# A quarter of the B products of one batch moved from GpSimd to ScalarE and TensorE

## The chip, the cores and the metric

The kernel runs on one core of one Trainium2 chip. The metric is the device time of one execution in microseconds (us). The core has five engines that run side by side, each through its own instructions in a fixed order: PE (TensorE, matrix products), DVE (VectorE), ACT (ScalarE), POOL (GpSimd) and SP (SyncE, which here only issues DMAs). They meet through semaphores.

## What is computed

The input is x, 4 batches of 384 channels by 32 by 32 pixels (1024 positions). Layer 0 normalises x and runs a selective scan over it in four directions ("turns": rows, columns, and both backwards). Layer 1 is attention with a window over the 1024 tokens of a batch and a mixture of four experts, two to a token. Cut to the scan, which is where the change lies:

```python
dts, Bs, Cs = (x_dbl[:, :, :R], x_dbl[:, :, R:R + N], x_dbl[:, :, R + N:])      # R = 12, N = 16
dts = jnp.einsum('bkrl,kdr->bkdl', dts, dt_projs_weight)
A = -jnp.exp(A_logs).reshape(K, D, N)
dt = jax.nn.softplus(dts + dt_projs_bias[None, :, :, None])
def step(h, inp):                      # over the 1024 positions
    dtt, ut, bt, ct = inp
    dA = jnp.exp(dtt[..., None] * A)
    h = h * dA + (dtt * ut)[..., None] * bt[:, :, None, :]
    y = jnp.einsum('bkdn,bkn->bkd', h, ct)
    return (h, y)
```

For each batch, direction and channel there are 16 states. A state needs a decay exp(dt A), an input dt u B, the recurrence over positions, and a product of its result with C; the products of the 16 states of a channel are then added up.

## The kernel before

**Slots.** The work of the scan is cut into 768 slots. A slot is a tile of 128 partitions by 1024 positions, and its partitions hold 32 channels by 4 states (`SG = 4`). A block is 32 channels, and takes `NG = 4` slots, one for each group g of four states. Three tiles `t` of 128 channels with four blocks `j` each make a turn: 48 slots; four turns make a batch. The slots of two neighbouring blocks alternate, so eight slots (g = 0, 0, 1, 1, 2, 2, 3, 3) belong together, and the order is the same on all engines.

**What a slot costs on each engine:**

- SP loads `spreads[n, 0]` (dt, in a `dts` buffer) and `spreads[n, 1]` (dt times u, in a `dtu` buffer), each copied to the 4 states of its channel on the way, once for a block; and rows of B and C (`bcs`), broadcast, once for a turn and g.
- ACT (`decay`): `dA = exp(dt A)`, from SBUF into a PSUM tile. There are two such tiles `das_`.
- POOL (`times_b`): `z = dtu * B`, SBUF to SBUF. There are seven `z` tiles. It may be at most `AHEAD = 3` slots ahead of the scan.
- DVE (`scan`): the recurrence, with `da` from PSUM and `z` from SBUF, in one instruction.
- DVE or POOL (`times_c`): the product with C. On POOL (`on_pool`), the scan writes into `z`, and `da` comes free at once. On DVE the scan writes into `da`, which comes free after the product.
- PE (`fold_y`): for two slots at a time, four products with `fold` add up the states. After that the two `z` come free.

**dt.** `half_step` makes dt for half of the positions of one tile: a product on PE, then softplus by ACT in pieces. Its last step adds three terms: in the first batch PE does that by three products with the identity (`by_pe`), in the others DVE by two additions. Then DVE makes dt times u, and SP stores both to DRAM (`dtr`), from where `spread` loads them.

**The rest.** When a batch has been scanned, its attention runs (`tokens`), then the routing, and the experts' blocks (`hidden`, `output`; 73 blocks in all) in three packs: batch 0, batches 1 and 2, batch 3. They share the engines with the scan of the next batches. What follows the scan of batch 3 has no scan beside it. `prepare` lays weights out afresh in DRAM during the first turns; `wts` is a stock of eight buffers for weights, which is little used in the first batch.

**Order.** All this is written as Python generators. A planner (`Machine`) with estimated costs decides, while the program is built, which instruction each engine gets next; the chip then runs these fixed lists. Ties are decided by a seeded random number (`SEED`), so a change of seed, or of any step, draws the order of the whole program afresh. `EARLY` and `LATER` are handicaps in the planner's choice.

Of the kernel before, what the change touches and what calls it, by code (L numbers as in the profile page):

```python
# [11 lines left out]
F32 = mybir.dt.float32  # L12
AF = mybir.ActivationFunctionType
ALU = mybir.AluOpType
# [375 lines left out]


PATIENCE = 3.0
TIE, SEED = 0.1, 53
SOON = 0.5
WINDOW, COLD = 3.413, 1.9
MARGIN, QUEUES = 1.0, ("sp",)
# [4 lines left out]
def conv_attn_hybrid(  # L401
# [159 lines left out]
    have = set()  # L561
    count_of = dict(scan=0, times=0)
    pe, act, dve, pool, sp = m.pe, m.act, m.dve, m.pool, m.sp

    def place_of(s):

# [100 lines left out]
    def group_norm(b):  # L667
# [91 lines left out]
        def project(pair):  # L759
            if not b and pair:  # L760
                yield lambda: count_of["times"] > 0
            xos = yield from (zs_ if b else wts).take("xo", n=2)
            given = xos
            xos = [xo[:, :L] for xo in xos]
            for h in range(NH):
                if b:
                    us = yield from us_.take("ux", n=2)
                    uv = [us[t // NH][:, ts(t % NH, HB)] for t in range(T)]
                    for t in range(T):
                        yield from sp.dma_start(uv[t], udr[b][t][:, ts(h, HB)])  # L770
                else:
                    uv = [first_u[t][:, ts(h, HB)] for t in range(T)]
                ps = yield from banks.take("ps_x", 0)
                pv = ps[: 2 * XR, :]
                mm = Calls()
                for t in range(T):
                    mm.matmul(
                        pv, xw_sb[:, t, 2 * pair : 2 * pair + 2, :].rearrange("p k r -> p (k r)"),
                        uv[t], start=t == 0, stop=t == T - 1,
                    )  # L780
                yield from pe.all(mm)
                if b:
                    us_.give(*us)
                    yield from act.copy(xos[0][: 2 * XR, ts(h, HB)], pv)
                yield from (copy if b else dve.tensor_copy)(
                    xos[1][: 2 * XR, :].rearrange("r (w h) -> r h w", h=HH)[:, ts(h, HH // NH), :],
                    pv.rearrange("r (h w) -> r h w", w=WW),
                )
                if not b:
                    yield from act.copy(xos[0][: 2 * XR, ts(h, HB)], pv)  # L790
                banks.give(ps)
            if not b and pair == 0:
                xds[0] = [xos[1][:R, ts(h, HB)] for h in range(NH)]
            for n in (1, 0):
                r = slice((1 - n) * XR, (2 - n) * XR)
                yield from sp.dma_start(xdr[b][2 * pair + n], xos[n][r, :])
                have.add(("x", b, 2 * pair + n))
            if b:
                zs_.give(*given)
            elif pair:  # L800
                wts.give(*given)
            else:
                wts.give(given[0])
                first_u.append(given[1])
# [26 lines left out]
    def state_rows(c):  # L831

        for i, (b, k) in enumerate(turns):
            for g in range(NG):
                yield lambda: ("x", b, k) in have
                bc = yield from (cs_ if c else bs_).take("bc")
                r = R + c * NS + SG * g
                yield from sp.dma_start(
                    bc, xdr[b][k, r : r + SG, :].unsqueeze(0).to_broadcast([32, SG, L])
                )  # L840
                bcs[i, g, c] = bc
# [23 lines left out]
    def half_step(i, t, h, u, dtr):  # L865
        b, k = turns[i]
        bias, c = dtb_sb[:, k, t : t + 1], ts(h, HB)
        by_pe = b == 0
        e, dt, *more = yield from eds.take("ed", n=3 if by_pe else 2)
        w = yield from banks.take("ps_dt", 0)  # L870
        yield from pe.matmul(w, dtws[i][h][:, ts(t, P)], xds[i][h], start=True, stop=True)
        yield from act.activation(e, w, AF.Abs, bias=bias)
        yield from act.activation(dt, w, AF.Relu, bias=bias)
        yield from act.activation(e, e, AF.Exp, scale=-1.0)
        if by_pe:
            yield from act.activation(w, e, AF.Identity, bias=minus, scale=-1.0)
            yield from dve.scalar_tensor_tensor(e, w, 1.0, e, ALU.add, ALU.add)
            yield from act.activation(more[0], w, AF.Ln, scale=-1.0)
            mm = Calls()
            for n, part in enumerate((dt, e, more[0])):  # L880
                mm.matmul(w, ident, part, start=n == 0, stop=n == 2)
            yield from pe.all(mm)
        else:
            yield from act.activation(w, e, AF.Identity, bias=1.0)
            yield from dve.scalar_tensor_tensor(e, w, -1.0, e, ALU.add, ALU.subtract)
            yield from act.activation(w, w, AF.Ln)
            yield from dve.tensor_tensor(w, w, e, ALU.subtract)
            yield from dve.tensor_tensor(w, w, dt, ALU.add)
        if k % 2:
            v = slice(h * (WW // NH), (h + 1) * (WW // NH))  # L890
            yield from dve.tensor_tensor(
                e.rearrange("p (w h) -> p w h", h=HH),
                w.rearrange("p (w h) -> p w h", h=HH), colmajor(u)[:, v, :], ALU.mult,
            )
        else:
            yield from dve.tensor_tensor(e, w, u[:, c], ALU.mult)
        yield from act.copy(dt, w)
        banks.give(w)
        yield from sp.dma_start(dtr[1][:, c], e)
        yield from sp.dma_start(dtr[0][:, c], dt)  # L900
        eds.give(e, dt, *more)

    def spread(c):

        for n, (i, t, j) in enumerate(blocks):
# [4 lines left out]
            )  # L910
            spreads[n, c] = dst

    def times_b():
        for s in range(NSLOT):
            n, g = place_of(s)
            i = blocks[n][0]
            yield lambda: (
                (n, 1) in spreads and (i, g, 0) in bcs and s <= count_of["scan"] + AHEAD
            )
            z = yield from zs_.take("z", 0)  # L920
            yield from pool.tensor_tensor(z, spreads[n, 1], bcs[i, g, 0], ALU.mult)
            zs[s] = z
            count_of["times"] += 1
            if g == NG - 1:
                dtus.give(spreads.pop((n, 1)))
            if n % NB == NB - 1:
                bs_.give(bcs.pop((i, g, 0)))

    def decay():
        for s in range(NSLOT):  # L930
            n, g = place_of(s)
            i, t, j = blocks[n]
            yield lambda: (n, 0) in spreads and "a4" in have
            da = yield from das_.take("dA")
            yield from act.activation(
                da, spreads[n, 0], AF.Exp, scale=a4[:, turns[i][1], t, j, g : g + 1]
            )
            das[s] = da
            if g == NG - 1:
                dts.give(spreads.pop((n, 0)))  # L940
# [14 lines left out]
    def scan():  # L955

        for s in range(NSLOT):
            n, g = place_of(s)
            i = blocks[n][0]
            yield lambda: s in zs and s in das  # L960
            z, da = zs[s], das.pop(s)
            on_pool = count_of["times"] >= min(s + AHEAD, NSLOT) and m.clock["pool"] < m.clock["dve"] + LEAD
            h = z if on_pool else da
            if turns[i][1] >= 2:
                yield from dve.tensor_tensor_scan(
                    h[:, ::-1], da[:, ::-1], z[:, ::-1], 0.0, ALU.mult, ALU.add
                )
            else:
                yield from dve.tensor_tensor_scan(h, da, z, 0.0, ALU.mult, ALU.add)
            count_of["scan"] = s + 1  # L970
            if s % SP == 0:
                m.spawn(fold_y(n), EARLY)
            if on_pool:
                das_.give(da)
                m.spawn(times_c(s, h, True))
            else:
                yield from times_c(s, h, False)
# [336 lines left out]
    def route(at_part):  # L1314
# [67 lines left out]
        nb = rp.tile([P, NE], F32, tag="nb", name="nb")  # L1382
        slot = rp.tile([P, PT, NE], F32, tag="slot", name="slot", bufs=1)
        if opens:
            total = rp.tile([P, NE], F32, tag="total", name="total")
            done = rp.tile([P, NE], F32, tag="done", name="done")
            start = rp.tile([P, NE], F32, tag="start", name="start")
            counts[PACK[b]] = total, done, start
            mm.scalar_tensor_tensor(
                slot, bcast(base_e, PT), float(P), cn[:, :PT, :], ALU.mult, ALU.add  # L1390
# [254 lines left out]
    with tc.manual_schedule():  # L1645
# [3 lines left out]
            m.spawn(group_norm(b), EARLY)  # L1649
        for gen in (turn_loads(), time_steps(), state_rows(0), state_rows(1), spread(1), spread(0)):  # L1650
            m.spawn(gen, EARLY)
        for gen in (decay(), times_b(), scan()):
            m.spawn(gen)
        m.spawn(layer1(), EARLY)
# [58 lines left out]
```

## Time and profile before

| | |
|---|---|
| time, median of 3 runs | 3725.83 us (3725.29 to 3727.22) |
| the profiled execution's own time | 3715.52 us |
| its span, first to last instruction | 3713.8 us |
| busy PE / DVE / ACT / POOL | 2999.4 / 2858.1 / 2217.3 / 2802.2 us |
| first scan / last scan ends | 61.1 us / 3029.6 us |
| turns 1 to 4 (first batch) | 167.3, 161.6, 166.6, 162.4 us |
| turns 5 to 8 (second batch) | 202.6, 213.4, 182.3, 175.7 us |
| third and fourth batch | 786.9 and 749.7 us |

The turns are read from the trace: DVE's 768 scans in order of time, 48 to a turn, from the start of a turn's first scan to the start of the next turn's. In a row of the profile stand the line, engine, operation, tiles (out<-in), shapes and count; then the busy time of the group, the mean duration of one in ns, the engine's idle time just before them, and what ended it. Most steps are recorded through one helper, so lines L155 and L166 hold nearly all, and a row is told by its tiles. An engine overlaps the end of an instruction with the start of the next, so a group's busy time over its count can be less than the mean duration.

### The profile page before, as it was taken

Reading aid. Unit: us, or ns where it says so; the run is one execution under the profiler, and the core shown is the slowest. Engines: PE = TensorE matmul, PEld = TensorE weight load, DVE = VectorE, ACT = ScalarE, POOL = GpSimd, SP = SyncE. Lnnn points to the kernel's source line nnn. Section 1 sums busy time; section 2 is a strip of 40 time slices with the busy share of each in tenths; the row PEclk is TensorE's granted clock in tenths of the full one; section 3 lists DMA queues with packets and bytes.
Section 4 is the critical chain, followed back from the end, with each engine's and each line's share of the span. In section 5 each row is a group of like instructions: output and inputs, shape, how many; then the busy total and the mean of one; then the engine's idle time right before and its main releaser. Section 6 shows DMA issues by size and latency. Waiting matters only on the chain.

```text
span 3713.8 us, 49879 instructions
## 1 busy us (share of the span) xinstructions
PE 2999.4 (81%) x15793; PEld 1820.8 (49%) x15793; DVE 2858.1 (77%) x3282; ACT 2217.3 (60%) x3984; POOL 2802.2 (75%) x1466
## 2 busy tenths in 40 slices
PE   5566565578788888896778898988888889999997
PEld 2111110045455545463445555655555558877886
DVE  4999999989888999999888999898898963331001
ACT  4454455477676777775667577876667644542221
POOL 3999988989899988999888799998899950112001
PEclk8766776688799989896778899987999999999997
DMA  5876887635489988864369999553899874469995
GB/s 201 288 279 238 276 301 251 207 124 165 150 298 347 368 323 329 304 211 151 124 218 311 328 338 347 194 178 133 291 320 328 321 262 156 153 222 321 321 322 174
DMA packets 396472, 944.51 MB, mean 254 GB/s; under 512 B 50064, under 2 KB 181256, under 8 KB 396208
## 3 DMA queue, kind: packets, MB, share of 16 engines
q1 hardware_dynamic: 384600, 915.73, 70.7%
q0 software_dynamic: 8192, 25.17, 2.0%
q8 instruction: 126, 2.06, 0.2%
q14 instruction: 138, 1.13, 0.1%
q10 hardware_dynamic: 3416, 0.41, 0.1%
HBM read 765.26 MB, written 194.77 MB: 259 GB/s over the span
## 4 chain that ended last, share of the span: by engine, by line
PE 34%; DVE 14%; ACT 10%; POOL 8%; DMA 7%; issue 6%; SPq 1%; another core or an unknown queue 1%; DVEq 0%; POOLq 0%; ACTq 0%
PE y_ff L166 9%; PE ps_hid L166 9%; POOL z L155 6%; DVE dA L155 5%; DVE z L155 4%; PE ps_y L166 3%; PE ps_qk L166 3%; ACT dA L155 2%; PE ps_pr L166 2%; DMA dtr<-ed 2%; PE ps_o L166 2%; ACT ed L155 1%; DVE ps_r L166 1%; PE ps_c L166 1%; ACT L166 1%
## 5 line engine op out<-in xcount | busy, mean ns | idle before, releaser
L155 POOL TENSOR_TENSOR z<-dts,bc 128x1024 f32<-128x1024 f32 x768 | 1792.9, 2363 | 112.5 <-PE ps_y L166 55.7
L155 ACT ACTIVATE dA<-dts,a 128x1024 f32<-128x1024 f32 x768 | 855.3, 1118 | 500.5 <-DVE z L155 486.0
L155 DVE TENSOR_TENSOR_SCAN dA<-dA,z 128x1024 f32<-128x1024 f32 x418 | 955.9, 2287 | 88.9 <-ACT dA L155 75.1
L166 PE MATMUL ps_y<-z,fold 128*32 128x512 f32 x3072 | 665.9, 732 | 321.4 <-POOL z L155 177.1
L155 POOL TENSOR_TENSOR z<-z,bc 128x1024 f32<-128x1024 f32 x350 | 821.3, 2360 | 106.7 <-DVE z L155 105.3
L155 DVE TENSOR_TENSOR_SCAN z<-dA,z 128x1024 f32<-128x1024 f32 x350 | 786.3, 2275 | 38.3 <-ACT dA L155 36.2
L166 PE MATMUL y_ff<-w_sb,hs 128*128 128x384 f32 x1752 | 671.1, 524 | 49.7 <-ACT hs L166 48.6
L166 PEld LDWEIGHTS ps_hid<-xbt,w_sb 128*128 128x128 f32 x5256 | 634.5, 196 | 131.0 <-issue 47.5
L166 PE MATMUL ps_hid<-xbt,w_sb 128*128 128x128 f32 x5256 | 658.8, 282 | 23.1 <-DMA w_sb<-wl 6.7
L155 DVE TENSOR_TENSOR z<-dA,bc 128x1024 f32<-128x1024 f32 x418 | 510.3, 1221 | 19.1
L166 PEld LDWEIGHTS y_ff<-w_sb,hs 128*128 128x128 f32 x1752 | 333.9, 204 | 297.9 <-ACT hs L166 72.9
L155 ACT ACTIVATE hs<-ps_hid,bb 128x128 f32<-128x128 f32 x876 | 262.0, 365 | 337.8 <-PE ps_hid L166 249.6
L166 PEld LDWEIGHTS ps_y<-z,fold 128*32 128x32 f32 x3072 | 91.6, 118 | 694.6 <-POOL z L155 322.9
L155 POOL DMA_INDIRECT cb<-ysdr,idx x64 | 61.9, 967 | 311.8 <-DMA ysdr<-yb 277.1
L166 POOL TENSOR_TENSOR rn<-rn,half 128x1 f32<-128x1 f32 x96 | 53.1, 553 | 229.6 <-DVE rn L166 188.3
L155 DVE COPY yb<-y_ff 128x384 f32<-128x384 f32 x23 | 12.8, 557 | 243.6 <-PE y_ff L166 242.0
L155 POOL DMA_INDIRECT xsdr<-tks,idx x64 | 65.4, 1022 | 110.0 <-DVE idx L166 48.2
L155 ACT ACTIVATE ed<-ps_dt,dtb_sb 128x512 f32<-128x512 f32 x192 | 123.5, 681 | 38.0 <-PE ps_dt L155 24.1
L155 ACT COPY ed<-ps_dt 128x512 f32<-128x512 f32 x96 | 56.2, 585 | 116.0 <-DVE ed L155 115.8
L166 PE MATMUL ps_dt<-ed,ident 128*128 128x512 f32 x144 | 82.7, 729 | 45.0 <-ACT ed L155 45.0
L155 PE MATMUL ps_dt<-xd,dtw_sb 12*128 12x512 f32 x180 | 108.7, 780 | 9.3 <-DVE gate L166 3.0
L311 ACT ACT_TABLE_LOAD x79 | 101.4, 1283 | 13.0 <-DMA gb_sb<-in_gb_dram 11.6
(220 smaller groups left out, 3509.8 us busy)
## 6 DMA issues: line engine op xcount, KB each, us to landing
w_sb<-wl SPq DMA_DIRECT2D x584, 576.0 KB
dts<-dtr SPq DMA_DIRECT2D x384, 512.0 KB
bc<-xdr SPq DMA_DIRECT2D x128, 512.0 KB
dtr<-ed SPq DMA_DIRECT2D x192, 256.0 KB
yp<-ydr SPq DMA_DIRECT2D x96, 256.0 KB
ydr<-yp SPq DMA_DIRECT2D x96, 256.0 KB
ub<-udr SPq DMA_DIRECT2D x45, 512.0 KB
xsdr<-zero SPq DMA_DIRECT2D x12, 1536.0 KB
```

The source lines that it names most:

```text
L155: return getattr(self.real, op)(*a, **k)
L166: getattr(self.real, op)(*a, **k)
L311: self.nc.scalar.add_instruction(mybir.InstLoadActFuncSet(name=self.nc.get_next_instruction_name(), act_func_set_id=EXP_LN_SET,))
```

## The change

In turns 2 to 4 of the first batch, the slots with g = 3 (36 of 768: every fourth) get their `z` in another way. `turn_inputs` loads dt times u once more as 128 channels by 1024 positions (`nat`), turns it round on PE in 128x128 pieces so that positions lie on partitions, and copies it to SBUF (`back`). There B is one number to a partition for each state, so ACT multiplies by it with its `scale` operand, 128 elements at a time, and writes the four states side by side with a step of four elements (`zt`). `decay` then has PE turn eight pieces of 128x128 back, into the PSUM tile in which the decay would have been; the decay itself is written by ACT into the SBUF tile `z`, and the scan takes its operands from the swapped places. The columns of B are made in `project`, by products with parts of the identity (`cols`). POOL's product, and the broadcast load of B for g = 3 of these turns, fall away. POOL's lead in the condition for a product with C on POOL is one slot shorter in these turns. The first tile's sums of the first turn go from PE to DVE. Three small tiles of the routing get one buffer in place of two, and the seed changes.

```diff
-TIE, SEED = 0.1, 53
+TIE, SEED = 0.1, 5
+TURNED, SOONER = 3, 24
...
+    def turned(i, g):
+
+        return 0 < i < KG and g == TURNED
...
+            if not b:
+                for n in (1, 0):
+                    k = 2 * pair + n
+                    if k == ORDER[0]:
+                        continue
...
+                    r = (1 - n) * XR + R + SG * TURNED
+                    mm = Calls()
+                    for a in range(NT):
+                        mm.matmul(
+                            ps[:, SG * a : SG * a + SG], xos[n][: 2 * XR, ts(a, P)],
+                            ident[: 2 * XR, r : r + SG], start=True, stop=True,
+                        )
+                    yield from pe.all(mm)
+                    yield from act.copy(b_cols[0][:, k * NT * SG : (k + 1) * NT * SG], ps[:, : NT * SG])
...
+                if not c and turned(i, g):
+                    continue
...
-        by_pe = b == 0
+        by_pe = b == 0 and i + t > 0
...
+    def turn_inputs():
+        for i in range(1, KG):
+            k = turns[i][1]
+            for t in range(T):
+                yield lambda: (i, t) in dtrs and ("columns", k) in have and len(dtrs) > T
+                yield lambda: count_of["scan"] >= (i * T + t) * TS - SOONER
+                nat = yield from wts.take("nat")
+                yield from sp.dma_start(nat[:, :L], dtrs[i, t][1])
+                yield m.settled(nat)
+                back = yield from wts.take("back")
+                for h in range(NH):
+                    ps = yield from banks.take("ps_tu")
+                    mm = Calls()
+                    for a in range(NT // NH):
+                        mm.transpose(ps[:, ts(a, P)], nat[:, h * HB + a * P : h * HB + a * P + P], ident)
+                    yield from pe.all(mm)
+                    yield from act.copy(back[:, ts(h, HB)], ps)
+                    banks.give(ps)
+                wts.give(nat)
+                tiles = []
+                for a in range(NT):
+                    if a % 2 == 0:
+                        z = yield from wts.take("zt")
+                        tiles.append(z)
+                    v = z[:, a % 2 * SG * P : (a % 2 + 1) * SG * P].rearrange("p (d s) -> p s d", s=SG)
+                    for n in range(SG):
+                        yield from act.activation(
+                            v[:, n, :], back[:, ts(a, P)], AF.Copy, scale=b_cols[0][:, (k * NT + a) * SG + n :][:, :1]
+                        )
+                wts.give(back)
+                across[i, t] = tiles
...
     def times_b():
...
+            if turned(i, g):
+                yield lambda: (n, 0) in spreads and (s - 2 in das or count_of["scan"] >= s - 1)
             z = yield from zs_.take("z", 0)
-            yield from pool.tensor_tensor(z, spreads[n, 1], bcs[i, g, 0], ALU.mult)
+            if turned(i, g):
+                _, t, j = blocks[n]
+                yield from act.activation(
+                    z, spreads[n, 0], AF.Exp, scale=a4[:, turns[i][1], t, j, g : g + 1]
+                )
...
     def decay():
...
+            if turned(i, g):
+                yield lambda: (i, t) in across
+                da = yield from das_.take("dA")
+                mm = Calls()
+                for a in range(NT):
+                    at = a % 2 * SG * P + j * P
+                    mm.transpose(da[:, ts(a, P)], across[i, t][a // 2][:, at : at + P], ident)
+                yield from pe.all(mm)
+                das[s] = da
...
-            on_pool = count_of["times"] >= min(s + AHEAD, NSLOT) and m.clock["pool"] < m.clock["dve"] + LEAD
+            on_pool = count_of["times"] >= min(s + AHEAD - (0 < i < KG), NSLOT) and m.clock["pool"] < m.clock["dve"] + LEAD
             h = z if on_pool else da
+            of, to = (z, da) if turned(i, g) else (da, z)
...
-            total = rp.tile([P, NE], F32, tag="total", name="total")
-            done = rp.tile([P, NE], F32, tag="done", name="done")
-            start = rp.tile([P, NE], F32, tag="start", name="start")
+            total = rp.tile([P, NE], F32, tag="total", name="total", bufs=1)
+            done = rp.tile([P, NE], F32, tag="done", name="done", bufs=1)
+            start = rp.tile([P, NE], F32, tag="start", name="start", bufs=1)
...
+        m.spawn(turn_inputs(), LATER)
```

More of the change, by code (lines that the diff above doesn't have):

```diff
@@ L791, in project @@
                 banks.give(ps)
+            if not b:
[3 more added lines that the diff above has]
+                        continue
+                    if not b_cols:
+                        b_cols.append((yield from wts.take("cols")))
+                    ps = yield from banks.take("ps_bc", 0)
+                    r = (1 - n) * XR + R + SG * TURNED
[8 more added lines that the diff above has]
+                    banks.give(ps)
+                    have.add(("columns", k))
             if not b and pair == 0:
@@ L911, in spread @@
             spreads[n, c] = dst
+    across = {}
+    b_cols = []
+    def turn_inputs():
[15 more added lines that the diff above has]
+                    yield from act.copy(back[:, ts(h, HB)], ps)
+                    banks.give(ps)
+                wts.give(nat)
[11 more added lines that the diff above has]
+                across[i, t] = tiles
+        wts.give(b_cols[0])
     def times_b():
@@ L917, in times_b @@
             yield lambda: (
-                (n, 1) in spreads and (i, g, 0) in bcs and s <= count_of["scan"] + AHEAD
+                (n, 1) in spreads and (turned(i, g) or (i, g, 0) in bcs) and s <= count_of["scan"] + AHEAD
             )
+            if turned(i, g):
+                yield lambda: (n, 0) in spreads and (s - 2 in das or count_of["scan"] >= s - 1)
             z = yield from zs_.take("z", 0)
-            yield from pool.tensor_tensor(z, spreads[n, 1], bcs[i, g, 0], ALU.mult)
+            if turned(i, g):
[3 more added lines that the diff above has]
+                )
+                if g == NG - 1:
+                    dts.give(spreads.pop((n, 0)))
+            else:
+                yield from pool.tensor_tensor(z, spreads[n, 1], bcs[i, g, 0], ALU.mult)
             zs[s] = z
@@ L925, in times_b @@
                 dtus.give(spreads.pop((n, 1)))
-            if n % NB == NB - 1:
+            if n % NB == NB - 1 and not turned(i, g):
                 bs_.give(bcs.pop((i, g, 0)))
@@ L932, in decay @@
             i, t, j = blocks[n]
+            if turned(i, g):
[7 more added lines that the diff above has]
+                das[s] = da
+                if j == JB - 1:
+                    wts.give(*across.pop((i, t)))
+                continue
             yield lambda: (n, 0) in spreads and "a4" in have
@@ L961, in scan @@
             z, da = zs[s], das.pop(s)
-            on_pool = count_of["times"] >= min(s + AHEAD, NSLOT) and m.clock["pool"] < m.clock["dve"] + LEAD
+            on_pool = count_of["times"] >= min(s + AHEAD - (0 < i < KG), NSLOT) and m.clock["pool"] < m.clock["dve"] + LEAD
             h = z if on_pool else da
+            of, to = (z, da) if turned(i, g) else (da, z)
             if turns[i][1] >= 2:
                 yield from dve.tensor_tensor_scan(
-                    h[:, ::-1], da[:, ::-1], z[:, ::-1], 0.0, ALU.mult, ALU.add
+                    h[:, ::-1], of[:, ::-1], to[:, ::-1], 0.0, ALU.mult, ALU.add
                 )
             else:
-                yield from dve.tensor_tensor_scan(h, da, z, 0.0, ALU.mult, ALU.add)
+                yield from dve.tensor_tensor_scan(h, of, to, 0.0, ALU.mult, ALU.add)
             count_of["scan"] = s + 1
```

## The prediction

> **What bounds the kernel now.** I read first the page's chain that ended last (its shares are spread over all engines: PE 34%, DVE 14%, ACT 10%, POOL 8%, so it settles nothing), then busy times by stretches, then the waits there, then the rows that price the parts.
>
> ```profile
> 228.40:390.00 161.60, 98.19 (x256) 21.15 (x252) 151.34 (x93) 78.47 (x90) 154.30 (x67) 0.67 0.74 256
> 390.00:556.60 166.60, 100.11 (x288) 23.35 (x288) 156.00 (x109) 88.61 (x100) 150.70 (x67) 0.71 0.83 284
> 556.60:719.00 162.40, 89.60 (x220) 14.31 (x220) 158.23 (x103) 79.67 (x94) 151.05 (x67) 0.65 0.67 228
> sum 490.60, PE 287.90 PEld 58.81 DVE 465.58 ACT 246.75 POOL 456.05; mean PE 95.97 PEld 19.60 DVE 155.19 ACT 82.25 POOL 152.02
> ```
> ```profile
> 1493.00:1679.30 186.30, 159.81 (x898) 98.75 (x896) 172.86 (x188) 142.29 (x262) 177.63 (x92) 0.89 0.73 253
> 2879.20:3029.60 150.40, 134.83 (x777) 82.59 (x776) 145.20 (x85) 100.26 (x162) 144.69 (x63) 0.95 0.84 298
> ```
>
> After the time, the columns are busy PE, PEld, DVE, ACT, POOL, then granted clock, DMA share, GB/s. In turns 2 to 4 (490.6 us) DVE works 94.9% and POOL 93.0% of the time, ACT only 50%. So DVE and POOL together set the pace, and the slots' C products, which either can make, level them. The last two rows are turns 9 and 16, for comparison.
>
> ```profile
> POOL z L155 <- DVE z L155: 20.5, 9, 6.5
> DVE dA L155 <- ACT dA L155: 5.2, 6, 1.7
> PE ps_y L166 <- POOL z L155: 95.5, 44, 7.1
> PE ps_dt L166 <- ACT ed L155: 14.7, 6, 4.4
> ACT dA L155 <- DVE z L155: 180.5, 102, 3.8
> ```
>
> These are waits in the same stretch (total, times, longest). POOL's waits are mostly for DVE; ACT waits 180.5 us for DVE to give a PSUM tile back. PE waits with its folds for POOL: idle time that today costs nothing.
>
> ```profile
> L155 POOL TENSOR_TENSOR z<-dts,bc 128x1024 f32<-128x1024 f32 x146 | 339.1, 2362 | 12.7 <-DMA xdr<-xo 5.9 <-PE ps_y L166 4.5 <-DMA ydr<-yd 2.3
> L155 POOL TENSOR_TENSOR z<-z,bc 128x1024 f32<-128x1024 f32 x52 | 121.5, 2355 | 21.4 <-DVE z L155 20.5 <-DVE ps_gm L166 0.9
> L155 DVE TENSOR_TENSOR_SCAN z<-dA,z 128x1024 f32<-128x1024 f32 x54 | 120.8, 2273 | 2.4 <-ACT dA L155 2.4
> L155 DVE TENSOR_TENSOR z<-dA,bc 128x1024 f32<-128x1024 f32 x92 | 112.6, 1224 | 7.7
> ```
> ```profile
> L166 PE MATMUL ps_p<-ident,s 128*128 128x128 f32 x360 | 59.4, 310 | 11.2 <-ACT pt L155 3.4 <-DVE mx L155 1.8 <-ACT yl L155 1.5
> L155 ACT ACTIVATE hs<-ps_hid,bb 128x128 f32<-128x128 f32 x876 | 262.0, 365 | 337.8 <-PE ps_hid L166 249.6 <-issue 71.0 <-remote 4.4
> L155 ACT ACTIVATE yd<-un,dsum 128x1024 f32<-128x1024 f32 x9 | 18.8, 2090 | 0.0
> L155 ACT ACTIVATE un<-un,g 128x1024 f32<-128x1024 f32 x9 | 11.2, 1239 | 10.9 <-DMA un<-in_x_dram 8.7 <-issue 2.2
> ```
>
> The first four are the prices of a B product, a C product on POOL, a scan and a C product on DVE; the last four, from the whole run, are the nearest rows for what is added.
>
> **POOL and DVE, turns 2 to 4.** POOL loses 36 B products: 36 x 2.362 = 85.0 us. The two programs' orders show what takes the place: of these turns' 144 C products DVE made 31, 31 and 29 and now makes 20, 20 and 22. So 29 go to POOL: 29 x 2.355 = 68.3 us. POOL nets 16.7 us less (439.4 busy), DVE 29 x 1.224 = 35.5 us less (430.1 busy). POOL becomes the fuller of the two. If it keeps its whole idle time (34.5 us), the stretch shrinks by 16.7; if DVE keeps its own (25.0), by 35.5. POOL's idle time is mostly waiting for DVE, which now has the room, so I let the fuller engine work the share that the fuller one works now: 439.4 / 0.949 = 463.0 us, a gain of 27.6.
>
> **ACT.** Added: 288 multiplications of 128x128. The row of hs gives 262.0 / 876 = 0.30 us each back to back and 0.365 alone; yd, which writes with a step, costs 2.090 - 1.239 = 0.851 us per 1024 elements more than un, or 0.106 per 128. So 0.30 to 0.47; I take 0.36 (the step here is four elements, yd's is 32), 104 us. With 18 copies of 128x512 at 0.585 (the row ed<-ps_dt), 10.5 us, ACT comes to 246.8 + 114 = 361 us of 463, 78% (at the bounds 74% and 85%). The 36 exponentials only change the tile that they write. In turn 9 ACT works 142.3 / 186.3 = 76%, with POOL at 95% and DVE at 93%, so this is hidden behind ACT's 180.5 us of waits for DVE; where an exponential that DVE needs comes late behind a multiplication, that costs 0.36.
>
> By the Trainium skill ("ScalarE: Activation LUTs", What ACT_TABLE_LOAD costs), an activation has a fixed price of 186 ns and 93 for a pointer operand, with 0.833 ns an element, so that cutting work into 128 elements pays mostly for the start: an estimate of 0.386 us alone, 0.29 back to back. That speaks against this form; the hs row agrees within its two readings, and 288 x 0.386 = 111 us would change the load by 7 us, still hidden.
>
> **PE.** Added: 72 + 288 transposes at 59.4 / 360 = 0.165 us, 59 us in all, 1.32 for a slot's eight. PE's 288 us leave room. What matters is the new wait: a turned slot's scan waits for its eight transposes, and these for the PSUM tile, free one scan (2.28 us) earlier, and for whatever stands before them in PE's list. In the new order a fold stands directly in front of 20 of the 36, but nearly all fold slots four or more back, or ones whose C product DVE has made. Five (three that fold a product of POOL's from three slots back, two from two back) can be late. A fold takes 1.92 us (four products at 0.48 in the timeline at 602 us), so with three hops of 0.1 between engines (as from the end of ACT's dA at 61.00 to the scan at 61.10) 1.92 + 1.32 + 0.3 - 2.28 = 1.3 us each. Behind the transposes queue the next folds, which give `z` tiles back to POOL. Three more stand behind products for dt, which wait up to 4.4 us for ACT (row ps_dt <- ACT ed). So 5 x 1.3 = 6.5, up to 6.5 + 3 x 4.4 = 20; with nothing late, 0. I take 7 us.
>
> The granted clock is 0.65 to 0.71 here. The Trainium skill ("TensorE: Matmul & The Clock Gate", Part 4: PE-mode transpose) says that transposes do not count as busy for the clock gate, so that the added work would leave the folds at 1.92 us; if it raised the clock to full, a fold would take some 0.67 x 1.92 = 1.3 us, and the 7 us would be 3.
>
> **DMA, and SP.** Nine loads of 512 KB come (nat), three of 512 KB go (B rows): 3.1 MB more, 12 us at the stretch's 256 GB/s, where DMA is busy 67 to 83%. Nine issues of 0.6 us go into SP's list ahead of some loads of dts. A slot's dtu is needed 30 slots after the load is allowed, about 96 us, so nothing: bounds 0 and 3 us. The table loads in the two orders fall from 158 to 146, 15 us of ACT over the run, hidden.
>
> **The start.** With DVE making the first sums, the wait of DVE for PE (36.11 to 40.95 us) becomes two additions of 0.69: 3.4 us earlier. But eight column products now stand on PE before the first dt product, and wait for ACT's second copy (ends 30.90, dt product now at 30.35): 16 instructions at 0.16 to 0.27 us (row ps_xt<-gw_sb) make it 3.2 to 5 us later. -0.2 to +1.6 us; I take 0.
>
> **After the first batch** everything hangs on its last fold, so the gain is carried along. The new order has 48 experts' blocks begun before the last scan, as before; so the tail, where PE is busy over 90%, has the same load. C products by DVE go from 297 to 304 there; DVE's instructions of turns 5 to 15, priced by their rows, sum to 3 us more, POOL's 7 products less. Order drawn afresh: +2, with 10 either way, for equal numbers of slots took 774, 787 and 750 us in three batches.
>
> **Sum.** -27.6 + 7 + 2 = -18.6 us. The profiled execution's 3715.5 becomes 3696.9; that execution lies 10.3 below the median of the runs, so on the median's footing 3725.8 - 18.6 = 3707. A difference under 0.2% (7.5 us) could not be told from none.
>
> **Rivals.**
>
> *Slower: PE's list holds up the scan.* If the fold in front of the transposes is late as a rule, because POOL, now the fuller engine, finishes its C products late, all 36 turned slots lose 1.3 us: 47 us; -27.6 + 47 + 2 = +21, or 3747. It decides once the mean loss passes 27.6 / 36 = 0.77 us. For it speaks PE's 95.5 us of waiting for POOL in this stretch; against it, that the folds in front are old ones. Chance 0.19.
>
> *No change: POOL keeps its idle time.* Gain 16.7 only, less 12 us of late transposes and 2 later: 3723. For it: POOL's B products still must be made ahead in slot order, and with 28 C products a turn it has no slack. Chance 0.15.
>
> *More: DVE was the pace-maker.* The stretch shrinks by DVE's 35.5, nothing is late, the new order costs nothing: 3690. For it: in turn 16 both work 96 to 97% of the time, so they can run levelled; 439.4 / 0.965 = 455 is the same gain. Chance 0.18.
>
> **How the numbers follow.** The forecast has the rest, 0.48, between about 3695 and 3716 (the two bounds of the transposes and of the redrawn order). Faster: 0.48 + 0.18 = 0.66; same 0.15; slower 0.19. The range takes in the largest gain with some of the order's 10 us, 3684, and two thirds of the way from no change to the slow rival, 3740.
>
> **What would show it.** Right: turns 2 to 4 take some 470 us; POOL 93 to 95% busy, DVE a little less, ACT near 78%; zt near 0.36 us; DVE's waits for PE at turned slots sum to under 10 us; the rest keeps its length. Wrong: a row of DVE waiting for PE's dA of tens of us; ACT's exponentials late behind zt; POOL's idle time as large as now; or later batches that differ by more than 10 us.

## The result, and the profile after

| | before | changed |
|---|---|---|
| median of 20 runs each | 3726.16 us | 3709.45 us |
| lowest to highest | 3710.31 to 3740.31 | 3697.61 to 3728.32 |
| ratio, 95% interval | | 0.9958 (0.9947 to 0.9970) |
| the profiled execution's own time | 3715.52 us | 3714.82 us |

The changed kernel is faster by 0.42%, 15.6 us; the interval spans 11 to 20 us. The forecast was 3707. The two profiled executions differ by only 0.7 us, since that of before lay 10 us under its median and that of the changed kernel 5 us over its own. So each program was profiled once more, and lengths of stretches are compared between pairs of profiles.

The changed kernel by stretches, as before: turns 2, 3 and 4 and their sum.

```profile
229.30:377.80 148.50, 95.35 (x362) 36.62 (x360) 137.59 (x82) 102.68 (x168) 146.91 (x64) 0.80 0.77 271
377.80:540.50 162.70, 111.24 (x408) 43.21 (x408) 143.61 (x99) 119.11 (x201) 145.58 (x64) 0.76 0.84 300
540.50:701.40 160.90, 98.28 (x344) 30.52 (x344) 150.07 (x95) 102.90 (x171) 152.15 (x67) 0.74 0.70 244
sum 472.10, PE 304.87 PEld 110.35 DVE 431.28 ACT 324.69 POOL 444.65; mean PE 101.62 PEld 36.78 DVE 143.76 ACT 108.23 POOL 148.22
```

Turns 2 to 4 fell from 490.6 to 472.1 us. DVE has 34.3 us less to do and POOL 11.4 us less; ACT has 78 us more. POOL is now the fuller of the two, at 94.2%. The waits in that stretch:

```profile
DVE dA L155 <- POOL z L155: 9.8, 5, 4.3
DVE ed L155 <- ACT ps_dt L155: 5.2, 4, 2.2
DVE z L155 <- PE dA L166: 5.0, 5, 1.6
DVE dA L155 <- PE dA L166: 4.9, 4, 1.5
DVE z L155 <- ACT dA L155: 4.5, 5, 1.7
```
```profile
ACT dA L155 <- DVE z L155: 61.5, 38, 7.1
PE dA L166 <- DVE z L155: 45.1, 16, 10.1
```

The new wait, DVE for the transposes (PE dA), is there twice, for scans that write `z` and scans that write `dA`: 9.9 us at 9 of the 36 turned slots. ACT's waits for DVE fell from 180.5 to 61.5 us, more than the 78 us of new work on it. The new work itself, in the same stretch:

```profile
L155 ACT ACTIVATE zt<-back,cols 128x128 f32<-128x128 f32 x240 | 81.8, 504 | 12.7 <-PE dA L166 12.7
L166 PE MATMUL dA<-ident,zt 128*128 128x128 f32 x288 | 58.6, 374 | 45.3 <-DVE z L155 45.1
L155 DVE TENSOR_TENSOR_SCAN z<-z,dA 128x1024 f32<-128x1024 f32 x25 | 56.3, 2273 | 5.1 <-PE dA L166 5.0
```

A multiplication lasts 504 ns on average, but the 240 keep ACT busy for only 81.8 / 240 = 0.34 us each: in a row, the next begins 0.293 us after the one before (median of 188). (The other 48 of the 288 run in turn 1.) Eight transposes take 58.6 / 36 = 1.63 us, where 1.32 was forecast. A scan with its operands swapped costs what it did, 2273 ns.

### The profile page after: what moved, and what is told of

Read it like the earlier page. It is cut to its first block, busy times and chain, and to the rows that moved or that the text cites. A ratio compares the mean times of both kernels' runs of the same rounds, so it can differ in the third digit from the quotient of the medians.

```text
span 3713.1 us, 50939 instructions
## 1 busy us (share of the span) xinstructions
PE 3039.6 (82%) x16171; PEld 1905.3 (51%) x16171; DVE 2838.2 (76%) x3270; ACT 2302.1 (62%) x4293; POOL 2772.6 (75%) x1452
## 5 line engine op out<-in xcount | busy, mean ns | idle before, releaser
L155 POOL TENSOR_TENSOR z<-dts,bc 128x1024 f32<-128x1024 f32 x732 | 1711.4, 2365 | 123.4 <-PE ps_y L166 55.5
L155 ACT ACTIVATE dA<-dts,a 128x1024 f32<-128x1024 f32 x732 | 814.4, 1118 | 429.5 <-DVE z L155 401.7
L155 POOL TENSOR_TENSOR z<-z,bc 128x1024 f32<-128x1024 f32 x372 | 874.5, 2364 | 109.9 <-DVE z L155 96.6
L155 DVE TENSOR_TENSOR_SCAN dA<-dA,z 128x1024 f32<-128x1024 f32 x385 | 880.6, 2287 | 95.4 <-ACT dA L155 68.2
L166 PE MATMUL ps_y<-z,fold 128*32 128x512 f32 x3072 | 608.6, 705 | 219.1 <-POOL z L155 161.2
L166 PE MATMUL ps_hid<-xbt,w_sb 128*128 128x128 f32 x5256 | 664.2, 283 | 29.7 <-DMA w_sb<-wl 8.6
L155 DVE TENSOR_TENSOR z<-dA,bc 128x1024 f32<-128x1024 f32 x396 | 483.4, 1221 | 15.2
L155 DVE TENSOR_TENSOR ps_dt<-ps_dt,ed 128x512 f32<-128x512 f32 x148 | 102.3, 691 | 11.5 <-ACT ps_dt L155 9.2
L166 PE MATMUL ps_o<-v,pt 128*128 128x64 f32 (+1 forms) x720 | 103.7, 303 | 3.8 <-DVE mx L155 2.7
```

What stands on the lines that cost most here:

```text
L155: return getattr(self.real, op)(*a, **k)
L166: getattr(self.real, op)(*a, **k)
```

## Experiments

All stretches below are from profiles. "Blocks" counts the experts' blocks (of 73) that PE has begun when the last scan ends; the tail is what follows that. "C" counts DVE's C products among the 144 of turns 2 to 4.

| kernel | C | DVE busy, turns 2-4 | POOL busy | turns 2-4 | blocks | tail |
|---|---|---|---|---|---|---|
| before, two profiles | 91 | 465.6, 465.3 | 456.1, 456.8 | 490.6, 489.6 | 48 | 684, 672 |
| before, seed 5 | 92 | 466.5 | 456.5 | 491.7 | 45 | 723 |
| before, shorter lead | 84 | 456.5 | 473.6 | 481.0 | 47 | 699 |
| before, POOL relieved | 91 | 465.4 | 407.6 | 490.4 | 48 | 673 |
| before, DVE relieved | 91, 30 of them cut | 436.4 | 453.4 | 475.7 | 48 | 673 |
| before, both relieved | 91, 30 of them cut | 436.0 | 407.3 | 467.4 | 48 | 672 |
| changed, no slot turned | 81 | 453.5 | 475.5 | 482.5 | 47 | 690 |
| changed, lead as before | 81 | 454.3 | 399.3 | 480.9 | 44 | 736 |
| changed, two profiles | 62 | 431.3, 431.9 | 444.7, 445.0 | 472.1, 469.1 | 48 | 692, 677 |
| changed, transposes twice | 62 | 432.9 | 445.0 | 490.3 | 48 | 676 |
| changed, multiplications twice | 62 | 435.4 | 438.4 | 561.0 | 48 | 674 |
| changed, shorter lead everywhere | 64 | 434.6 | 439.5 | 478.5 | 47 | 697 |

These runs were on chips where the kernel before took 3710 us, so ratios are to before on the same chip.

**Both programs once more.** No edit.

> The kernel before, unchanged, profiled once more, to see how far the stretches of one program differ between executions. In the first profile turns 2 to 4 took 490.6 us, the 12 turns after them 2310.6 and what follows the last scan 684.2. If those lengths belong to the program, they come back within 3 us; if the 8 us by which the new kernel's third batch stretch and tail were longer is chance of an execution, some of them move by 5 to 10 us.

> The changed kernel, unchanged, profiled once more. Its first profile has turns 2 to 4 at 472.1 us, the turns after them at 2320.0 and the tail at 691.7, and was 5 us over its median, while that of before was 10 us under its own. If the gain is made in turns 2 to 4 and the rest is chance, turns 2 to 4 come back at 472 within 3 us, and turns 5 to 16 with the tail nearer to before's 2994.8 than to 3011.7.

Turns 2 to 4 came back at 489.6 and 469.1 us. Turns 5 to 16 took 2323.1 us in the second profile of before (2310.6 in the first), and 2314.3 in the changed kernel (2319.9); the tails were 672.2 and 677.3 us. So turns 2 to 4 came back within 3 us, as expected, while turns 5 to 16 and the tail differ by up to 15 us between executions of one program. The extra length of the tail in the first profile of the changed kernel was mostly of that kind.

**Nothing turned.**

```diff
-        return 0 < i < KG and g == TURNED
+        return False
...
-            if not b:
+            if False:
                 for n in (1, 0):
                     k = 2 * pair + n
                     if k == ORDER[0]:
...
-        m.spawn(turn_inputs(), LATER)
```

> The changed kernel with no slot turned: POOL makes all B products again, no columns of B, no transposes; the first tile's sums on DVE, the shorter lead in turns 2 to 4, the single buffers and the new seed stay. Theory L (the moved products make the gain): turns 2 to 4 go back to 485 to 491 us and the whole to 3720 to 3730, ratio to before 0.9985 to 1.001. Theory O (first sums, lead and redrawn order make it): 3708 to 3715, ratio 0.995 to 0.997.

The ratio was 0.9996 (0.9984 to 1.0008): as theory L says for the whole. But turns 2 to 4 took 482.5 us, less than either theory's 485 to 491 for them: some 7.6 us of the 19.5 (means 490.1 and 470.6) come without any turned slot. DVE makes 81 C products there for 91, with POOL at 98.6%. The whole shows none of it: the tail took 689.8 us, for 684.2 and 672.2 before. PE has nearly as much to do in it (4034 instructions, for 4015 and 4023), so why it is longer is not shown.

**The seed alone.**

```diff
-TIE, SEED = 0.1, 53
+TIE, SEED = 0.1, 5
```

> The kernel before with the seed of the changed one, 5 for 53, and nothing else: only the order is drawn afresh. Theory L: within 10 us of before either way, turns 2 to 4 at 487 to 494 us (DVE makes 92 of 144 C products, as before). Theory O: 3705 to 3715, most of the measured gain of 16 us.

Neither theory: 1.0098 (1.0082 to 1.0114), 37 us slower, with turns 2 to 4 at 491.7, as theory L has them. All of the loss is in the tail, whose busy times (PE first) are:

```profile
3021.40:3744.80 723.40, 676.36 (x4285) 549.55 (x4283) 142.45 (x502) 231.61 (x667) 81.30 (x113) 0.96 0.73 247
```
```profile
3029.60:3713.80 684.20, 642.31 (x4015) 522.48 (x4014) 139.10 (x492) 221.99 (x634) 79.51 (x112) 0.94 0.72 240
```

The second is the kernel before. With seed 5, 45 blocks are begun by the last scan, not 48, so PE has 270 more instructions (x4285 for x4015) to run in a stretch where it is busy 94% of the time. The table goes the same way: 48 blocks, a tail of 672 to 692 us; 47, 690 to 699; 45, 723; 44, 736. From 48 to 45 and 44 that is some 15 us a block; between 47 and 48 it says little, since a block that has hardly begun counts whole. The order's draw can therefore be worth more than the change itself, and much of it is in a number that can be read from the built program.

**ACT's work doubled.**

```diff
                         yield from act.activation(
                             v[:, n, :], back[:, ts(a, P)], AF.Copy, scale=b_cols[0][:, (k * NT + a) * SG + n :][:, :1]
                         )
+                        nc.scalar.activation(
+                            v[:, n, :], back[:, ts(a, P)], AF.Copy, scale=b_cols[0][:, (k * NT + a) * SG + n :][:, :1]
+                        )
```

> The changed kernel with each of the 288 multiplications on ACT made twice, one right after the other; the order of all else is unchanged. In the profiles of the changed kernel the 288 keep ACT busy for 97.8 us (0.34 each), 325 us of the 472 of turns 2 to 4. Theory H (ACT's added work lies behind its waits for DVE): ACT goes to about 410 us in turns 2 to 4, these become 3 to 8 us longer, and the whole under 0.2%. Theory A (ACT's order holds up the exponentials that DVE waits for): a large part of the 98 us comes through, turns 2 to 4 at 500 us or more, the whole 0.7% longer or more.

1.0278 (1.0257 to 1.0300), turns 2 to 4 at 561 us: theory A's numbers. But the test was heavier than meant. The rows of the two copies in turns 2 to 4, and five of them in order of time (start, duration):

```profile
L971 ACT ACTIVATE zt<-back,cols 128x128 f32<-128x128 f32 x240 | 126.7, 528 | 7.8
L155 ACT ACTIVATE zt<-back,cols 128x128 f32<-128x128 f32 x240 | 119.9, 499 | 11.9 <-PE dA L166 11.9
```
```profile
299.61 0.51 ACT L155 ACTIVATE zt<-back,cols 128x128 f32<-128x128 f32 x1
300.14 0.53 ACT L971 ACTIVATE zt<-back,cols 128x128 f32<-128x128 f32 x1
300.46 0.49 ACT L155 ACTIVATE zt<-back,cols 128x128 f32<-128x128 f32 x1
300.99 0.53 ACT L971 ACTIVATE zt<-back,cols 128x128 f32<-128x128 f32 x1
301.31 0.50 ACT L155 ACTIVATE zt<-back,cols 128x128 f32<-128x128 f32 x1
```

Line L971 is the second copy. It starts 0.53 us after the first, which has then ended; the next pair's first copy starts 0.32 us after the second, and overlaps it. In the trace each second copy waits for a semaphore that the first sets (the two write the same place), so it is the program that keeps the two apart. Together the 480 keep ACT busy for 208.1 us, where the 240 took 81.8. (The two rows add up to more, since they overlap each other.) ACT's load rose by 120 us there (444.7 for 324.7), and 90 us came through; DVE's waits for ACT's `dA` rose from 6.8 to 84.3 us. So this order hid about 30 of the 120 us. For the work as it stands the waits decide: DVE waited for ACT's `dA` 6.8 us in the changed kernel and 7.6 before, so 78 us more on ACT added nothing to them.

**The transposes doubled.**

```diff
                 yield from pe.all(mm)
+                for op, o, kw in mm:
+                    getattr(nc.tensor, op)(*o, **kw)
                 das[s] = da
```

> The changed kernel with the eight transposes that turn a slot back made twice, right after each other; the order of all else is unchanged. A turned slot's input on PE becomes 1.3 us later. DVE waited for these transposes 9.9 and 7.2 us in two profiles. If most of the 36 have slack of over 1.3 us, as that suggests: turns 2 to 4 within 8 us of 470. If they have about 0.6 us (one scan of 2.28 less 1.32 and hops of 0.3), 0.7 us come through for each: 25 us, turns 2 to 4 at 495, the whole 0.6 to 0.7% longer.

1.0011 (0.9998 to 1.0024), 0.53% over the changed kernel; turns 2 to 4 at 490.3, 19.7 over the mean of the two profiles.

```profile
DVE z L155 <- PE dA L1014: 22.8, 16, 3.3
DVE dA L155 <- PE dA L1014: 6.9, 7, 1.6
```

DVE now waits 29.7 us at 23 slots, some 21 more than before the doubling. That is the second expectation, a little under it. The second eight end 1.2 us after the first on average (0.9 to 1.7), and 0.55 us come through for each of the 36, so the slots have about 0.65 us of slack on average. The new path costs little only because the eight transposes are short.

**One engine relieved, then both.** In the first, 36 B products become a fill of the tile (0.955 us); in the second each third of DVE's C products of these turns covers 64 columns; the third kernel has both. These parts of the computation are left out.

```diff
-            yield from pool.tensor_tensor(z, spreads[n, 1], bcs[i, g, 0], ALU.mult)
+            if 0 < i < KG and g == 3:
+                yield pool.ask("tensor_tensor", (z, spreads[n, 1], bcs[i, g, 0], ALU.mult), {})
+                nc.gpsimd.memset(z, 0.01)
+            else:
+                yield from pool.tensor_tensor(z, spreads[n, 1], bcs[i, g, 0], ALU.mult)
```
```diff
-            yield from dve.tensor_tensor(zs[s], h, bcs[i, g, 1], ALU.mult)
+            cut[0] += 0 < i < KG
+            if 0 < i < KG and cut[0] % 3 == 0:
+                yield dve.ask("tensor_tensor", (zs[s], h, bcs[i, g, 1], ALU.mult), {})
+                nc.vector.tensor_tensor(zs[s][:, :64], h[:, :64], bcs[i, g, 1][:, :64], ALU.mult)
+            else:
+                yield from dve.tensor_tensor(zs[s], h, bcs[i, g, 1], ALU.mult)
```

> The kernel before with its order unchanged, in which the 36 B products of g = 3 in turns 2 to 4 are left out and POOL fills the tile with a constant instead (about 1.0 us in place of 2.36, so some 50 us less on POOL in these turns); C products stay where they are. Theory L (POOL and DVE share the pace): turns 2 to 4 shrink by 10 to 20 us. Theory D (DVE alone sets the pace, and POOL's relief counts only because it lets C products move): 0 to 5 us.

> The same, and of the 91 C products that DVE makes in turns 2 to 4 each third is cut from 1024 to 64 columns (30 of them, about 1.0 us less each, so some 31 us less on DVE); the order is that of the kernel before. It takes the relief of both engines without any of the new work on ACT and PE. Both theories: turns 2 to 4 at 456 to 465 us. If it comes out at 470, the new work on ACT and PE costs nothing in the changed kernel; if it is lower, the difference is the price of the new waits.

> The kernel before, order unchanged, with only the cut of 30 of DVE's 91 C products in turns 2 to 4 from 1024 to 64 columns, and POOL's work whole (456 us busy of 490). With POOL relieved as well, the same cut gave 467.4 us. Theory D (DVE sets the pace, POOL only follows): 465 to 470 again. Theory P (POOL becomes the bound as soon as DVE is relieved, which the forecast assumed): 474 us or more.

POOL's relief alone, 49 us, is worth nothing: 490.4 us, ratio 0.9998 (0.9988 to 1.0008). It turns into waiting for DVE, 52.2 us where before had 20.5:

```profile
L155 POOL TENSOR_TENSOR z<-z,bc 128x1024 f32<-128x1024 f32 x53 | 123.8, 2351 | 56.5 <-DVE z L155 52.2 <-DVE ps_gm L166 4.2
```

DVE's relief alone, 29 us, is worth 14.4 us (475.7, against a mean of 490.1), and with POOL relieved too 22.7 us (467.4; ratio 0.9931, 0.9914 to 0.9947). The two rows, DVE alone and both:

```profile
227.80:703.50 475.70, 277.32 (x764) 58.14 (x760) 436.42 (x302) 246.62 (x284) 453.35 (x198) 0.67 0.76 263
225.40:692.80 467.40, 290.92 (x768) 59.70 (x768) 436.02 (x301) 246.21 (x284) 407.29 (x200) 0.67 0.78 269
```

DVE's busy time is the same in both, POOL's is not. So DVE sets the pace, and a POOL at 95% takes back 8 us of DVE's relief: theory D holds where POOL alone is relieved, theory P where DVE alone is. The 456 to 465 us expected with both relieved were not reached. The changed kernel, with DVE at 431.6 and POOL at 444.8, took 470.6: between these two kernels, which have none of the new work.

**The lead and the turned slots apart.** The first edit is on the kernel before, the second on the changed one, the third too.

```diff
-            on_pool = count_of["times"] >= min(s + AHEAD, NSLOT) and m.clock["pool"] < m.clock["dve"] + LEAD
+            on_pool = count_of["times"] >= min(s + AHEAD - (0 < i < KG), NSLOT) and m.clock["pool"] < m.clock["dve"] + LEAD
```
```diff
-            on_pool = count_of["times"] >= min(s + AHEAD - (0 < i < KG), NSLOT) and m.clock["pool"] < m.clock["dve"] + LEAD
+            on_pool = count_of["times"] >= min(s + AHEAD, NSLOT) and m.clock["pool"] < m.clock["dve"] + LEAD
```
```diff
-            on_pool = count_of["times"] >= min(s + AHEAD - (0 < i < KG), NSLOT) and m.clock["pool"] < m.clock["dve"] + LEAD
+            on_pool = count_of["times"] >= min(s + AHEAD - 1, NSLOT) and m.clock["pool"] < m.clock["dve"] + LEAD
```

> The kernel before with the shorter lead of POOL in turns 2 to 4 alone; POOL makes all B products; DVE makes 84 of these turns' 144 C products, for 91. Theory D: 7 x 1.22 = 8.5 us less on DVE, three quarters of it in the time: turns 2 to 4 at 482 to 485. Theory P: POOL has 16.5 us more, 472 of 490: no gain, 488 to 492.

> The changed kernel without the shorter lead: the 36 slots are turned, and DVE makes 81 C products in turns 2 to 4, for 62 with it and 91 before. Theory D: 10 x 1.22 = 12 us less on DVE than before, so that turns 2 to 4 take about 480 to 485 us although POOL is relieved of 85 - 24 = 61 us. Theory P: POOL's relief shows, 465 to 472.

> The changed kernel with the shorter lead in all turns: DVE makes 259 C products in turns 5 to 16, for 304, so that DVE has 45 x 1.22 = 55 us less and POOL 106 us more there; POOL is busy 89 to 95% of these turns and DVE 88 to 94%. Theory D: turns 5 to 16 shrink by 20 to 40 us, and the whole beats the changed kernel by 0.5 to 1%, if the tail's order is no worse. Theory P: POOL runs full, turns 5 to 16 become longer by 30 us or more.

The lead alone gave turns 2 to 4 of 481.0 us, the turned slots without it 480.9, both together 470.6 (means): 9.1, 9.2 and 19.5 us of gain. In all three, DVE's C products fell, by 7, 10 and 29. The two rows are the lead alone and the turned slots without it:

```profile
225.80:706.80 481.00, 291.31 (x772) 59.35 (x768) 456.54 (x295) 247.02 (x284) 473.60 (x206) 0.67 0.74 260
```
```profile
229.80:710.70 480.90, 312.53 (x1116) 105.80 (x1112) 454.33 (x292) 324.69 (x538) 399.25 (x173) 0.75 0.76 267
```

POOL works 473.6 us in one and 399.3 in the other, DVE 456.5 and 454.3, and the time is the same. That fits theory D (the lead alone is 1 us under its 482 to 485). Turned slots make room on POOL, and with the shorter lead as well the planner hands it 29 C products, for 10 and 7 with one of the two.

These three orders are drawn afresh, and a draw alone can move this stretch: the shorter lead everywhere has nearly the changed kernel's loads in turns 2 to 4 (DVE 434.6, POOL 439.5) and took 478.5 us, 8 more. So the two gains of 9 us are no exact shares, and the kernels with the order held fixed carry the argument.

The wholes show how much the gain of 0.42% hangs on the draw. The changed kernel with the lead as before has the same seed and the same 36 turned slots, but 44 blocks begun and a tail of 736; its one run took 3763.8 us, for 3710 before. The lead alone took 3702.2 in its one run.

The shorter lead everywhere did not beat the changed kernel: 1.0043 (1.0029 to 1.0058) to before. In turns 5 to 16 DVE had 49 us less (2037 for 2087) and POOL 106 more (2184 for 2078), and they took 2309.5 us, within the spread of one program. Neither theory's number came. That POOL, at 95%, took the gain back would fit the kernel with DVE alone relieved, but is not shown here. Turns 2 to 4 (478.5) were 8 us longer, and the tail (697, with 47 blocks) 12 us longer than the changed kernel's mean.

## Why the prediction was right

- **The sum in turns 2 to 4.** Forecast -27.6 + 7, so 470; measured 472.1 and 469.1. POOL's 439.4 and DVE's 430.1 us busy were measured at 444.7 and 431.3.
- **The mechanism.** "DVE and POOL together set the pace" is right only in part. POOL's own relief, 49 us, was worth nothing; DVE's, 29 us, was worth 14.4 us, and 22.7 with POOL relieved too. What the forecast had right is what the gain comes from: C products that leave DVE, and B products that leave POOL so that it has room for them.
- **The share of the fuller engine.** 94.9% was assumed and 94.2% found in that profile, 94.8 in the second. That the number held is partly luck: it is not a law, for POOL ran at 98.6% with nothing turned. What the runs show is DVE's busy time plus 24 to 44 us of waiting, in every kernel without doubled work. With the order held fixed it was 25 us before, 31 with both relieved, and 39 with DVE alone relieved.
- **The late transposes.** Forecast 5 slots at 1.3 us, 7 in all; measured 9 slots, 0.6 to 1.6 us, 9.9 in all, and 6 slots with 7.2 in the second profile. The size was right, the cause mostly another, so this term was partly luck. The forecast counted on folds that wait for POOL, and in its upper bound on products for dt that wait for ACT. A fold that had waited for POOL stood in front of 2 of the 9 (1.4 us), and of 2 of the 6 (3.4 us). At 10 of the other 11 the fold, or a product for dt, stood between the transposes of two neighbouring turned slots, and PE had not waited for its inputs:

```profile
319.65 1.94 PE L166 MATMUL dA<-ident,zt 128*128 128x128 f32 x8 [4.00 <-DVE z L155]
321.52 1.94 PE L166 MATMUL ps_y<-z,fold 128*32 128x512 f32 x8
321.63 2.29 DVE L155 TENSOR_TENSOR_SCAN z<-z,dA 128x1024 f32<-128x1024 f32 x1
323.39 1.97 PE L166 MATMUL dA<-ident,zt 128*128 128x128 f32 x8
325.45 2.29 DVE L155 TENSOR_TENSOR_SCAN dA<-z,dA 128x1024 f32<-128x1024 f32 x1 [1.53 <-PE dA L166]
```

  The first transposes start when DVE frees their tile; fold and second transposes then take 1.9 us each, and DVE's scan of 2.3 us is over before they are. Even with the transposes doubled only 23 of the 36 slots waited, so the rival in which all 36 lose 1.3 us did not come about.
- **ACT.** Forecast 0.36 us a multiplication and a load of 78%; measured 0.34 and 324.7 / 472.1 = 69%, in part since 48 of the 288 ran in turn 1. It was hidden. A term inside it was mis-sized: the write with a step of four elements was put at or under the price of yd's step of 32. A multiplication lasted 504 ns, 139 more than the row of hs (365), where the step of 32 gave 106; only the overlap with the next made 0.34 of it. The Trainium skill ("ScalarE: Activation LUTs", What ACT_TABLE_LOAD costs) had given 0.386 alone and 0.29 back to back, as an estimate; the trace has 0.504 for one and 0.293 from start to start in a row, so the second agrees and the first does not.
- **The start.** The first scan came at 55.0 and 57.0 us for 61.1 and 59.2, but turn 1 ended at 229.3 and 230.3 for 228.4 and 228.5: 1.4 us later in the mean, within the forecast's -0.2 to +1.6. Executions differ by as much (225.4 to 228.5 in five profiles with the order of before), so neither term is measured.
- **After the first batch.** That the gain is carried when 48 blocks are begun before the last scan, as before, fits the table. What was mis-sized is the spread of "10 either way" for an order drawn afresh: other orders came out 10 to 60 us worse in the tail. It did no harm here because the count of blocks had been read from the new order; for a program whose order was not known the range would have been far too narrow. Turns 5 to 16 took 2316.9 us before and 2317.1 after (means of two). With executions that differ by up to 15 us there and in the tail, that the median came within 2.5 us of the forecast of 3707 is luck. The 3695 to 3716 of the forecast's middle part do not follow from the bounds that it names: the order's 10 us alone give 3697 to 3717, the transposes' 0 to 20 alone 3700 to 3720.
- **The rival "POOL keeps its idle time"** had 3723. POOL's idle time fell from 34.5 to 27.4 us. The rival "DVE was the pace-maker" had the better mechanism, but its full 35.5 us need a POOL that is not full: with both relieved, 22.7 of 29 us came out, with POOL whole 14.4.

What stays open: the doubled multiplications were dear partly because each second copy waited for the first, and a copy that writes elsewhere was not tried. So how much more ACT could hide is not known; about 30 of 120 us were hidden there. Open too is how far another draw of the changed kernel's order would keep the 0.42%.

## What to carry to other kernels

When two engines share work that either can do, find out which one the other waits for, by relieving one at a time with the order held fixed; taking work from the follower pays only through what it then takes over. When a planner draws the whole order afresh, read from the built programs how much of the last stage is begun before the stage in front of it ends; here that count went with up to 60 us, four times the change. Compare stretches, not whole times, and profile a program twice to know which stretches are steady.

## What was not expected of the hardware

The granted clock in turns 2 to 4 rose from 0.68 to 0.77 with the transposes (0.77 and 0.78 in the two profiles; 0.75 with turned slots and the lead as before; 0.67 with nothing turned, and 0.67 in the kernel before with both engines relieved, which is as short), and a fold's matmul went from 879 to 771 ns. The Trainium skill ("TensorE: Matmul & The Clock Gate", Part 4: PE-mode transpose) says that transposes do not count as busy for the clock gate; the runs here, in which only the programs with added transposes show the higher clock, speak against it for these fp32 transposes, and the measurement decides. The rows list them as MATMUL with the identity, and do not show in which mode PE ran them. With the transposes doubled it stayed at 0.77, so the clock does not simply follow their number; with the multiplications doubled, which stretches these turns to 561 us, it was 0.69.

A write with a step of four elements made a multiplication on ACT last longer (504 ns, for 365 in the row of hs), but in a row one still starts 0.293 us after the other; hs starts 0.25 us apart.
